# A hybrid Mamba, attention and expert kernel: arrival times in the plan of its prologue, a clearing moved to block 32, a root moved to block 13

## The chip, the cores and the metric

The kernel runs on one core of one Trainium2 chip. The metric is the time of one execution on the device, in microseconds. A core has five engines with a queue each, which work in order: TensorE (PE), VectorE (DVE), ScalarE (ACT), GpSimd (POOL) and SyncE (SP, which here only issues transfers). They wait for each other through semaphores.

## The reference

The input is an image batch x of shape (4, 256, 32, 32), used as 4 batches of 256 channels by N = 1024 positions. Two layers follow each other. What the change touches lies in the first third of layer 0; the rest is listed so that its place is clear.

```python
# layer 0, on the group-normalised x (32 groups of 8 channels)
xn = layernorm(xs, norm_w, norm_b)                  # over the 256 channels, per position
xc = xn in NB = 4 parts of DM = 64 channels
# mamba, for each part and batch: DIN = 128, DS = 16 states, K = 4 taps
u, z = split(xs @ inw.T)
u = silu(causal_conv(u, convw) + convb)
xdbc = u @ xpw.T
dt = softplus(xdbc[:DTR] @ dtw.T + dtb)
h_t = exp(dt_t * A) * h_{t-1} + dt_t * u_t * B_t    # the scan, over 1024 positions
y = (h_t summed with C_t over the states) + u * Dp
xm = (y * silu(z)) @ outw.T + skip_scale * xc
# a gate over the parts of a batch
Q = pointwise(depthwise_3_taps(x_concat));  xg = sigmoid(Q) * xm
# then: convolutions, attention with 8 heads, gelu, a depthwise 3 x 3 convolution, a projection
# layer 1: attention with softmax over 1024 positions, then 16 experts of which each token takes 2
```

## The kernel before

**The stages.** A prologue loads the inputs, normalises x and makes the first part's scan inputs (until about 88 us). A scan loop of 256 blocks follows (to about 1032 us); then come the convolutions and attentions and the experts, which the change doesn't touch.

**The scan loop.** A block is 8 of the 128 inner channels of one part of one batch, with 16 states each: 128 rows by 1024 positions. 16 blocks make a part, 64 a batch. In block t, DVE multiplies dBu by B (L976) and scans (L979), and POOL multiplies by C (L980). PE spreads dt * u over the states for block t + 2 (`select`, L919) and sums the states of block t - 3 (`add_up`, L930 and L937). ACT takes the exponential for block t + 3 (`decay`, L912), on data which SP fetches for block t + 4 (L907). Steps of the next parts (`front`) and of parts just ended are issued at fixed blocks between these, in program order: whatever is issued at a block stands on its engine's queue at that place. A list `behind` of pairs (block, step) holds what the prologue leaves to the loop. For batch 3 these are the variances of the layernorm (`var_late`, L742 and L780), their reciprocal root (`root`, twelve small DVE steps, L676 to L683), a diagonal matrix of them on POOL (L755), and the multiplications that apply it (L763 to L770).

**The gate.** When the four parts of a batch are done, `module_gate` computes the gate in blocks 5, 21 and 37 after the batch's end. Its step 0 first runs for batch 0 in block 85. PE projects (L600) and ACT writes three shifted copies (L603) into a tile of 96 rows by 1026 columns, `late_gate[0]`, of which only 4 rows in each 32 are written. The remaining rows and the edge columns have to be zero, and are set so once, by POOL (L596). The tile lies in the space where x of batch 3 was held; the last to read it there are the variances of block 8.

**The prologue.** Its instructions are not in the order of the text. Each step is handed to a planner with `add`, with the engine, a cost in ns, what it reads and writes, and an optional `lag` until the result is there. The class `Plan` simulates the engines with these costs and issues the steps in the order of their simulated starts. So the costs fix only the order on each queue; on the chip, semaphores set the times. There are three kinds of steps: `main` (the chain of batch 0: `normalise(0)` and `first_front`), `fill` (`weights`: constants made from loaded weights) and `low` (the other batches and the first matmuls of part 1). A fill step goes ahead when it ends before the next main step could start, plus 300 ns; a low step may hold up a main step of its engine by up to 700 ns. When the plan shows a hole on PE, `between` puts filler matmuls of the identity with itself there (L630), one for 330 ns of planned hole. Each of them shows as two records in the profile.

`normalise(b)` runs through: sums over positions on DVE (L694, one for each half k of the channels), a matmul over groups (L695), the negative mean (L696), squares on ACT (L700), a matmul over groups (L703), the root on DVE (L706 and the lines from L676), scaling (L712); then the layernorm over channels: mean by matmul (L723), subtraction (L727), squares (L732), variances (L742), the root (L751), the diagonal (L755), its replication (L795), and the products (L801 to L813). `weights` makes m_cu (`taps`, L823, from m_in and convr), m_first (L825), m_wdt (L830 on PE, L832 on DVE, from m_xp and m_dt), pick (L833), ddiag and sdiag (L835, L836, from the constants) and aneg (L837, L838). `first_front` goes from m_first and the normalised batch 0 to dt and to U, the input of `select` (L855 to L892), with transfers of dt (L873) and of the parts of U (L885).

The input transfers are all issued by SP, in the order of the text, and none by the planner. The plan is told of them by steps on SP that issue nothing: one for each batch of x, with lags 9500, 13000, 16000 and 19000 ns. Of the weights it is told nothing, so they count as there at time 0; `taps` alone waits for batch 0 in the plan.

Of the kernel before, what the change touches and what calls it, by code (L numbers as in the profile page):

```python
# [17 lines left out]
B, C, HH, WW = 4, 256, 32, 32  # L18
# [149 lines left out]
class Plan:  # L168
# [85 lines left out]
    def run(self):  # L254
        time = dict.fromkeys(self.LATENCY, 0.0)
# [52 lines left out]
        while left:  # L308
            choices = []
            for e in time:  # L310
                pick = self.choose(e, time[e], best, start)
                pick, kind = pick if pick is not None else (None, None)
                low = best(e, self.low.get(e, ()), "low", 40, lambda op: op["at"] <= self.position)
                if low is not None and (pick is None or low[0] + (0 if e == "DVE" and kind == "fill" else low[1]["ns"]) <= pick[0] + self.slack):
                    pick, kind = low, "low"
                if pick is not None:
                    wait = self.rather_act if e == "DVE" and pick[1]["other"] is not None else 0
                    choices.append((pick[0] + wait, pick[1]["n"], e, kind, pick[1], pick[0]))
            if not choices:

                nxt = [op["at"] for k in ("fill", "low") for ops in kinds[k].values() for op in ops if op["at"] > self.position]
                assert nxt, "the plan has a circle"
                self.position = min(nxt)
                continue
            _, _, e, kind, op, t = min(choices, key=lambda c: c[:2])
            for bank in op["banks"] if op["take"] else ():
                places = [(f, i) for i, f in enumerate(free) if f is not None]
                i = max(i for f, i in places if f <= t) if kind == "low" and self.split else min(places)[1]
                free[i] = None
                bank.t, bank.i, bank.kind = self.banks[i], i, kind  # L330
                taken[kind] += 1
            if e == "PE" and self.between is not None and time[e] > 0:
                for _ in range(int((t - time[e] - 100) // 330)):
                    self.between()
            if e == "PE":
                t += self.TURN * (op["tiled"] != self.tiled)
                self.tiled = op["tiled"]
            second = op["second"]
            if second is not None:
                free_at = max([d["end"] + self.LATENCY[d["engine"]] for d in second["deps"] if d["engine"] != e] + [t])  # L340
                op["emit"]()
                second["emit"]()
                op["end"] = t + op["ns"]
                time[e] = second["end"] = max(op["end"] + second["ns"], free_at + op["ns"])
                if second["pos"] is not None:
                    self.position = max(self.position, second["pos"])
                for o in (op, second):
                    kinds[kind][e].remove(o)
                left -= 2
                continue  # L350
            if op["other"] is not None:
                kinds[kind]["DVE" if e == "ACT" else "ACT"].remove(op)
                if e == "DVE":
                    op["engine"], op["ns"], op["emit"] = op["other"]
            op["emit"]()
            op["end"] = t + op["ns"] + op["lag"]
            time[e] = t + op["ns"]
            for bank in op["banks"] if op["give"] else ():
                free[bank.i] = op["end"] + self.LATENCY[e]
                taken[bank.kind] -= 1  # L360
            if op["pos"] is not None:
                self.position = max(self.position, op["pos"])
            kinds[kind][e].remove(op)
            left -= 1
# [31 lines left out]
def body(tc, g, out):  # L396
    nc = tc.nc
# [8 lines left out]
    with pool("const", 1) as cp, pool("dram", 1, space=bass.MemoryType.DRAM) as drp, contextlib.ExitStack() as late:  # L406
# [46 lines left out]
        with pool("mconst", 1) as mc, pool("front", 1) as fp, pool("dts", 2, space=bass.MemoryType.DRAM) as dsp, pool(  # L453
# [135 lines left out]
            def module_gate(b, step):  # L589

                q12 = late_gate[0]
                if step == 0:
                    if b == 0:
                        nc.gpsimd.memset(q12, 0.0)  # L596
                    p = big()
                    for h in HALVES:
                        for k in range(CT):
                            mm(p[:96, h], qdw[:, k, :], XM[b][:, k, XL + h.start : XL + h.stop], start=k == 0, stop=k == CT - 1)  # L600
                    for j in range(3):
                        rows_j = slice(32 * j, 32 * j + NB)
                        act(  # L603
                            q12[rows_j, 2 - j : 2 - j + N], p[rows_j], AF.Identity,
                            bias=V("qdw_b")[rows_j] if j == 1 else 0.0, scale=1.0,
                        )
                else:
                    k, t = step - 1, late_gate[1]
                    p = big()
                    for h in HALVES:  # L610
                        mm(p[:, h], qpw[:, k * P : (k + 1) * P], q12[:, 1 + h.start : 1 + h.stop], start=True, stop=True)
                    act(t, p, AF.Sigmoid, bias=V("qpw_b", k), scale=1.0)
# [7 lines left out]
            with pool("scan", 6) as sp, pool("yps", 1, space=PSUM) as yps, pool("dps", 2, space=PSUM) as dps, pool("lnA", 1) as wp:  # L620
# [64 lines left out]
                def normalise(b):  # L685
# [90 lines left out]
                    if b == B - 1:  # L776
                        def var_late():
                            p = big()
                            var(p)
                            nc.scalar.copy(small[:, 0], each(p))  # L780
                        behind.extend([(8, var_late), (10, root), (15, diagonal)])
                        late(22, 23, 24, 25, 27)
                        return
                    add("PE", 3500, lambda: var(bank.t), SQUARE(b), (), bank, take=True)
# [32 lines left out]
                def weights():  # L817
# [3 lines left out]

                    def taps():
                        tt(m_cu, m_in[:, :, 0:DIN].unsqueeze(2).to_broadcast([P, CT, K, DIN]), convr, ALU.mult)  # L823
                    add("DVE", 1270, taps, XS(0), ["m_cu"])
                    add("ACT", 700, lambda: nc.scalar.copy(m_first[0:DM], m_cu[0:DM, 0]), ["m_cu"], ["m_first"])  # L825
                    bank = pre.bank()

                    def low_rank():
                        for nb in range(NB):
                            mm(bank.t[:, nb * DIN : (nb + 1) * DIN], m_xp[:, nb], m_dt[:, nb], start=True, stop=True)  # L830
                    add("PE", 2000, low_rank, (), (), bank, take=True)
                    add("DVE", 690, lambda: nc.vector.tensor_copy(m_wdt, bank.t.rearrange("p (n d) -> p n d", n=NB)), (), ["m_wdt"], bank, give=True)  # L832
                    add("DVE", 420, lambda: nc.vector.tensor_copy(pick, pickf), (), ["pick"])  # L833
                    for nb in range(NB):
                        add("DVE", 150, lambda nb=nb: ts(ddiag[:, nb], ident, V("dd", nb), None, ALU.mult))  # L835
                    add("DVE", 150, lambda: ts(sdiag, ident, V("skip"), None, ALU.mult))  # L836
# [109 lines left out]
                fronts = [None] + fronts  # L946
                behind = []

                for b in range(B):
                    add("SP", 0, lambda: None, (), XS(b), lag=(9500, 13000, 16000, 19000)[b])  # L950
                with pre.beside(-1, -1, -1):
                    weights()
                normalise(0)
# [1160 lines left out]
```

## Time and profile before

| | |
|---|---|
| median of 3 runs | 2792.1 us (2788.51 to 2798.54) |
| profiled execution, its own time | 2778.86 us |
| its span, first to last instruction | 2776.9 us |
| prologue, to the first L976 | 87.78 us |
| scan loop, first L976 to last L979 | 87.78 to about 1034 us |
| mean granted TensorE clock | 0.968 |

In the lines of the profile, PE is the matmul, PEld the loading of its weights, L12 line 12 of the kernel; times are us. In a timeline each line has start, duration, engine, line, operation, output <- input, the shape, and a count where several alike follow each other. In brackets stands how long the engine was idle before, and what ended that. Where the letter q follows an engine's name, it is the engine's sequencer, which issues transfers and handles semaphores.

Busy time by stage (of the windows 0 to 40, 40 to 86, 86 to 150 and 150 to 220 us), in us:

| stage | length | PE | DVE | ACT | POOL |
|---|---|---|---|---|---|
| prologue, first part | 40 | 26.24 | 22.28 | 9.25 | 1.02 |
| prologue, second part | 46 | 42.23 | 33.14 | 32.82 | 16.55 |
| loop, first blocks | 64 | 44.59 | 58.24 | 42.59 | 47.61 |
| loop, after them | 70 | 61.25 | 64.30 | 45.20 | 62.32 |

### The profile page before, as it was taken

How to read it: one execution, taken by the hardware profiler on the slowest of the kernel's cores; microseconds unless marked ns; L12 is line 12 of the kernel's file. 1: busy time of each engine (PE TensorE's matmuls, PEld its weight loads, DVE VectorE, ACT ScalarE, POOL GpSimd, SP SyncE). 2: the span in 40 equal slices, each digit the busy share in tenths (PEclk: the TensorE clock that was granted, in tenths of full speed). 3: DMA queues.
4: the chain of work that ended last, by engine and by line, in shares of the span. 5: the costliest groups of instructions: out<-in, count | busy, mean ns of one | idle time of the engine just before them, and what ended most of it. 6: DMA issues, size and time to landing. Idle time of an engine off the chain costs nothing. (4 is left out here: it accounts for less than half of the span.)

```text
span 2776.9 us, 38965 instructions
## 1 busy us (share of the span) xinstructions
PE 2510.8 (90%) x15320; PEld 1494.1 (54%) x15320; DVE 1997.8 (72%) x2261; ACT 1540.8 (55%) x2082; POOL 1321.6 (48%) x822
## 2 busy tenths in 40 slices
PE   7788887888888878999999999999999998899996
PEld 5322222222223224675655565664666667899996
DVE  6899998999999987777985997777594556111112
ACT  4766766767767734666865975784543433112120
POOL 1788887998898870000010010012343336566652
PEclk9999999999999999999999999999999998999998
DMA  4667766787767743000001000000000014555546
GB/s 148 171 157 184 174 168 165 182 191 187 175 172 180 192 115 106 9 5 22 22 1 39 9 2 9 9 17 16 1 16 8 12 35 121 173 140 141 128 100 182
DMA packets 95433, 269.58 MB, mean 97 GB/s; under 512 B 18694, under 2 KB 36726, under 8 KB 91920
## 3 DMA queue, kind: packets, MB, share of 16 engines
q1 hardware_dynamic: 66560, 202.52, 28.6%
q0 software_dynamic: 26512, 60.35, 8.6%
q10 hardware_dynamic: 2176, 4.19, 0.4%
q8 instruction: 122, 2.00, 0.3%
q14 instruction: 63, 0.52, 0.1%
HBM read 291.57 MB, written 42.80 MB: 120 GB/s over the span
## 5 line engine op out<-in xcount | busy, mean ns | idle before, releaser
L980 POOL TENSOR_TENSOR hs<-hs,bc 128x1024 f32<-128x1024 f32 x256 | 600.5, 2360 | 122.3 <-DVE hs L979 119.9
L979 DVE TENSOR_TENSOR_SCAN hs<-dA,dBu 128x1024 f32<-128x1024 f32 x256 | 585.4, 2287 | 36.8 <-PE pY L937 2.2
L1322 DVE TENSOR_REDUCE nm<-s 128x1 f32<-128x1024 f32 x256 | 301.5, 1218 | 94.0 <-PE s L1313 90.1
L1327 ACT ACTIVATE pr<-s,nm 128x1024 f32<-128x1024 f32 x256 | 285.7, 1122 | 94.4 <-DVE nm L1322 69.5
L912 ACT ACTIVATE dA<-dA,aneg 128x1024 f32<-128x1024 f32 x256 | 285.9, 1143 | 86.7 <-DMA dA<-ds 83.3
L976 DVE TENSOR_TENSOR dBu<-dBu,bc 128x1024 f32<-128x1024 f32 x256 | 309.3, 1208 | 12.7 <-PE dBu L919 12.6
L1391 POOL TENSOR_TENSOR b<-b 128x1024 f32<-128x1024 f32 (+1 forms) x15 | 29.6, 1972 | 590.3 <-ACT b L1387 590.2
L1341 PE MATMUL k<-const,pr 128*128 128x128 f32 x2048 | 270.2, 278 | 20.4 <-ACT pr L1327 6.3
L1341 PEld LDWEIGHTS k<-const,pr 128*128 128x128 f32 x2048 | 226.5, 142 | 109.3 <-issue 48.0
L919 PE MATMUL dBu<-U,pick 96*128 96x512 bf16 x512 | 158.7, 393 | 111.6 <-DVE hs L979 111.4
L1989 PE MATMUL s<-pT,b 128*128 128x128 f32 x1920 | 231.3, 277 | 7.4 <-DMA b<-we,intse 6.2
L1989 PEld LDWEIGHTS s<-pT,b 128*128 128x128 f32 x1920 | 227.1, 193 | 12.6 <-issue 5.8
L1993 DVE TENSOR_TENSOR pT<-pT,s 128x512 f32<-128x512 f32 x72 | 49.4, 686 | 233.7 <-ACT pT L1992 233.6
L937 PE MATMUL pY<-hs,const 128*32 128x512 f32 x768 | 198.3, 639 | 0.0
L919 PEld LDWEIGHTS <-pick 96*128 96x128 bf16 x512 | 41.1, 99 | 282.2 <-issue 158.8
L1345 ACT COPY pT<-k 128x512 f32<-128x512 f32 x288 | 156.7, 597 | 51.7 <-PE k L1341 51.4
L1345 DVE COPY pT<-k 128x512 f32<-128x512 f32 x224 | 144.7, 682 | 33.8 <-PE k L1341 30.9
L1313 PE MATMUL s<-b,b 32*128 32x512 f32 x512 | 166.2, 646 | 0.7 <-ACT pr L1327 0.6
L1313 PE MATMUL s<-b,qs 32*128 32x512 f32 x512 | 166.2, 646 | 0.0
L930 PE MATMUL pY<-hs,const 128*128 128x512 f32 x256 | 139.6, 672 | 10.2 <-ACT u L568 7.7
L1361 PEld LDWEIGHTS k<-pT,b 128*32 128x32 f32 x4096 | 107.6, 110 | 59.2 <-issue 27.1
L1361 PE MATMUL k<-pT,b 128*32 128x128 f32 x4096 | 129.9, 276 | 3.0 <-DVE pT L1345 3.0
(485 smaller groups left out, 4645.5 us busy)
## 6 DMA issues: line engine op xcount, KB each, us to landing
dA<-ds SPq DMA_DIRECT2D x256, 512.0 KB, 5.6
dq<-parts SPq DMA_DIRECT2D x15, 768.0 KB, 3.7
U<-dq SPq DMA_DIRECT2D x45, 256.0 KB, 6.9
ds<-dt SPq DMA_DIRECT2D x16, 512.0 KB, 3.0
b<-x SPq DMA_DIRECT2D x4, 1024.0 KB, 6.9
acc<-pr SPq DMA_DIRECT2D x8, 512.0 KB, 7.5
qs<-b SPq DMA_DIRECT2D x32, 128.0 KB, 2.2
xm<-x SPq DMA_DIRECT2D x4, 1024.0 KB, 5.4
```

The costliest lines, as they stand in the source:

```text
L912: act(dAs[t], dAs[t], AF.Exp, scale=aneg[:, c : c + 1])
L919: mm(dBus[t][:, h], pick[:, j % 4], state[t // NJ]["U"][:, j // 4, h], start=True, stop=True)
L976: tt(dBu, dBu, r["B"], ALU.mult)
L979: nc.vector.tensor_tensor_scan(hs, dAs.pop(t), dBu, 0.0, ALU.mult, ALU.add)
L980: nc.gpsimd.tensor_tensor(hs, hs, r["C"], ALU.mult)
L1313: mm(S[i][:, HALVES[h]], q, kT[rr, HALVES[h]], start=True, stop=True)
L1322: "DVE", 1130, lambda i=i, u=u: nc.vector.tensor_reduce(nms[u], S[i], AX.X, ALU.max, negate=True),
L1327: "ACT", 1100, lambda i=i, u=u, hd=hd: act(prs[u % 4], S[i], AF.Exp, bias=nms[u], scale=1.0, accum_out=rss[b % 2][:, k, qt, hd : hd + 1]), ...
L1341: nc.tensor.transpose(bank.t[:, j * P : (j + 1) * P], prs[u][:, c0 : c0 + P], ident)
L1345: 470, 598, lambda dst=dst, bank=bank: nc.scalar.copy(dst, bank.t), lambda dst=dst, bank=bank: nc.vector.tensor_copy(dst, bank.t),
L1361: mm(bank.t[i * HD : (i + 1) * HD, 0:P], v[:, 4 * jh + j, hd * HD : (hd + 1) * HD], pTs[m][jh][:, i, j * P : (j + 1) * P], start=(jh, j) = ...
L1989: mm(p12[:, a, c], wbufs[w][:, o : o + P], xT[:, k], start=k == 0, stop=k == CT - 1)
```

## The change

It has three parts. First, the planner is told when each input arrives: x in halves, with its own time for each, and m_in, m_dt, convr and pick. `taps`, `low_rank` and the cast of pick wait for them in the plan. The transfers and their order are the same. Second, fillers may now also stand before the first step of PE, counted from 4500 ns on. Third, two steps move in the loop: the clearing of the gate tile from block 85 to block 32, and batch 3's root from block 10 to block 13.

```diff
-            if e == "PE" and self.between is not None and time[e] > 0:
-                for _ in range(int((t - time[e] - 100) // 330)):
+            if e == "PE" and self.between is not None:
+                for _ in range(int((t - max(time[e], 4500) - 100) // 330)):
                     self.between()
...
                 q12 = late_gate[0]
                 if step == 0:
-                    if b == 0:
-                        nc.gpsimd.memset(q12, 0.0)
                     p = big()
...
-                        behind.extend([(8, var_late), (10, root), (15, diagonal)])
+                        behind.extend([(8, var_late), (13, root), (15, diagonal), (32, lambda: nc.gpsimd.memset(late_gate[0], 0.0))])
...
-                    add("DVE", 1270, taps, XS(0), ["m_cu"])
+                    add("DVE", 1270, taps, ["m_in", "convr"], ["m_cu"])
...
-                    add("PE", 2000, low_rank, (), (), bank, take=True)
+                    add("PE", 2000, low_rank, ["m_dt"], (), bank, take=True)
...
-                    add("DVE", 420, lambda: nc.vector.tensor_copy(pick, pickf), (), ["pick"])
+                    add("DVE", 420, lambda: nc.vector.tensor_copy(pick, pickf), ["pickf"], ["pick"])
...
-                for b in range(B):
-                    add("SP", 0, lambda: None, (), XS(b), lag=(9500, 13000, 16000, 19000)[b])
+                for keys, ns in (
+                    (XS(0, [0]), 8000), (XS(0, [1]), 9400), (["m_in"], 10500), (["m_dt"], 11500), (["convr"], 12200), (["pickf"], 13000),
+                    (XS(1, [0]), 15300), (XS(1, [1]), 16600), (XS(2, [0]), 17900), (XS(2, [1]), 19200), (XS(3, [0]), 20500), (XS(3, [1]), 21500),
+                ):
+                    add("SP", 0, lambda: None, (), keys, lag=ns)
```

## Prediction

> **What bounds the kernel now.** I read the page first: the row of shares, then the slices. PE is busy 90% of the span, but that is an average over stages: in slices 1 to 15 it is DVE that stands at 9.
>
> ```profile
> PE 2510.8 (90%) x15320; PEld 1494.1 (54%) x15320; DVE 1997.8 (72%) x2261; ACT 1540.8 (55%) x2082; POOL 1321.6 (48%) x822
> PE   7788887888888878999999999999999998899996
> DVE  6899998999999987777985997777594556111112
> ```
>
> All three edits lie in the first 430 us, so PE's bound behind slice 16 is untouched: time saved before it moves the whole rest forward, time saved off the path there is worth nothing. The chain that ended last covers only the final 50 us and says nothing here. So I went to the timeline of the prologue, engine by engine, and to DVE's list of waits in the scan loop.
>
> The prologue, DVE and PE (start us, duration us, what, in brackets the idle time before and its releaser):
>
> ```profile
> 13.03 0.42 DVE L833 CAST pick<-sz 96x512 bf16<-96x512 f32 x1 [12.12 <-DMA sz<-pick]
> 15.05 2.33 DVE L694 TENSOR_REDUCE gst<-hs 128x1 f32<-128x1024 f32 x2
> 13.46 8.67 PE L630 MATMUL pY<-const 128*128 128x128 f32 x60
> 21.98 0.28 PE L695 MATMUL pY<-gst,const 128*128 128x2 f32 x2
> 22.29 0.16 DVE L696 TENSOR_SCALAR gst<-pY 128x2 f32<-128x2 f32 x1 [3.78 <-PE pY L695]
> 83.51 3.70 PE L484 MATMUL mm<-xm,m_cu 64*128 64x512 f32 x8
> 87.14 1.04 PE L919 MATMUL dBu<-U,pick 96*128 96x512 bf16 x4
> 87.78 1.23 DVE L976 TENSOR_TENSOR dBu<-dBu,bc 128x1024 f32<-128x1024 f32 x1 [1.69 <-PE dBu L919]
> ```
>
> To be seen: batch 0's sums (L694) stand on DVE's queue behind a cast that waits for the last small transfer, pick, until 13.03, though x of batch 0 is there at about 9.3 (issued from 1.66, 7.2 us median to landing). Then PE comes to their matmul (L695) only at 21.98, because 30 filler matmuls (60 records, two to one) stand before it. The scan loop starts at 87.78.
>
> The loop, at block 85 and at its counterpart one batch later:
>
> ```profile
> 422.94 0.95 POOL L596 MEMSET xs<- 96x1026 f32 x1
> 423.93 1.02 ACT L603 ACTIVATE xs<-mm 4x1024 f32<-4x1024 f32 x1 [6.54 <-POOL xs L596]
> 427.14 3.43 PE L544 MATMUL mm<-u,m_bc 128*128 128x512 f32 x4 [7.86 <-ACT xs L603]
> 431.04 1.23 DVE L976 TENSOR_TENSOR dBu<-dBu,bc 128x1024 f32<-128x1024 f32 x1 [7.81 <-PE dBu L919]
> ...
> 656.66 1.01 ACT L603 ACTIVATE xs<-mm 4x1024 f32<-4x1024 f32 x1
> 658.98 1.21 DVE L976 TENSOR_TENSOR dBu<-dBu,bc 128x1024 f32<-128x1024 f32 x1
> ```
>
> The memset waits in POOL's backlog, ACT for the memset, PE for ACT, DVE for PE. DVE loses 7.81 us. One batch later there is no memset and no gap.
>
> **Part 1, the prologue's plan.** The planner orders each queue by its own costs; I use those for order only and take durations from rows. Now x, m_in, m_dt, convr and pick carry arrival times, so on DVE only ddiag, sdiag and aneg precede the sums; these need const and vec, there at about 4.5 (ACT's aneg starts at 4.57 on vec). The second half of x0 lands at 9.3, its sum takes 1.17 (2.33 for two): 10.5. L695 takes 0.28, so L696 comes at about 10.9 instead of 22.29: **11.3 us earlier**. Taps, pick and m_wdt (1.21 + 0.42 + 0.68) move behind it, into the 2.4 us in which ACT squares batch 0 (two L700 rows), starting with convr at 12.2 (3.08 + 9.1); m_wdt waits for low_rank, 11.5 + 2.04 = 13.5, and ends by 14.4. L706, at 25.82 before, then comes at 14.4: still 11.4 earlier.
>
> Fillers: the first PE step is planned at 10.8, so (10800 - 4500 - 100)/330 = 18 fillers stand before L695, starting with const at 4.5. In the trace the first 9 of the 30 took 3.5 us (0.39 each), later ones 0.20: 9 × 0.39 + 9 × 0.20 = 5.3, ending near 9.9, under the wait for x0. If all 18 stayed slow they would end at 11.5: a loss of 1.0. The Trainium skill (TensorE: Matmul & The Clock Gate, "What's actually happening") says that the array falls to half clock after about 3.4 us idle and needs as long to come back. That speaks against this change: with x1 to x3 landing from 15.3 to 21.5 as before, PE has holes early. The nearest row: L495 took 3.78 at 94.44 after a gap, where the same four passes take 1.98 warm (L544 at 431.68). One such relapse costs 1.8 by row, up to 3.4 by the rule; fillers sit in every planned hole, so I take 0 and keep 3.4 for the range.
>
> What of the 11.4 survives to the loop? The other batches' work fills holes at lower priority. It can start at 15.4 instead of 22.37, only 7 us earlier, so it falls 4.4 us further behind. Two effects. (i) The first chain loses interruptions: the four L727 of batch 1 and two L696 which now stand before L755 (42.07 to 44.60) are not ready any more: 2.5 us gained. (ii) Displaced PE work piles up at the end. From L723 (30.43, will be 19.1) to 87.14 PE spends 56.7 us, of which 3.8 are fillers, some 2.5 idle, 50.4 work. In the new order I find holes of about 2 (before the variances L742), 3 (root and diagonal of batch 0, 2.5 + 1.2 less small matmuls), 1.8 (before L855) and up to 4 (the first select waits for U, which needs some 7 us from the last part to landing, with work queued behind it): 7 to 11. The last L484 then ends at 19.1 + 50.4 + 7 to 11 = 76.5 to 80.5 instead of 87.1. But the loop no longer waits for all of it: the first selects stand before the L484 and only block 2's stands behind. Block 3 needs last L484, table load 1.28, silu 1.11, L495 2.0 to 3.8, select 0.6: from 80.5 that is 85.5 to 87.3, against 99.12 (its L976 now): 11.8 to 13.6 earlier; from 76.5 DVE itself binds, at some 84. **I take -12.5** (ends -6, if all lag stays, and -15).
>
> **Part 2, the memset.** Gone from block 85: ACT, idle from 417.4, takes its three L603 at once (3.14 us), PE's L544 comes at 420.6 instead of 427.14, and the select is done as DVE ends its scan at 423.2. The counterpart at 656 stands in the same phase (L603 0.1 before a scan begins) and DVE waits nowhere there, but 0.5 three blocks later. So 7.81 - 0.2: **-7.6** (7.0 to 7.8). At block 32 it adds 0.95 to POOL, behind that block's L980:
>
> ```profile
> 219.22 2.36 POOL L980 TENSOR_TENSOR hs<-hs,bc 128x1024 f32<-128x1024 f32 x1 [1.12 <-DVE hs L979]
> 222.83 2.36 POOL L980 TENSOR_TENSOR hs<-hs,bc 128x1024 f32<-128x1024 f32 x1 [1.25 <-DVE hs L979]
> ```
>
> POOL idles 1.25 there, which covers it; its last reader, the variances of block 8, is long done. Without cover: 0.95, and behind it only the next L980. Cost 0.
>
> **Part 3, the root** of batch 3, from behind block 10 to behind block 13 on DVE.
>
> ```profile
> 129.85 0.58 DVE L676 TENSOR_SCALAR smalls<-smalls 128x8 f32<-128x8 f32 x1 [1.21 <-ACT smalls L780]
> 130.47 2.27 DVE L677 CAST smalls<-smalls 128x8 f32<-128x8 int32 x1
> 133.19 1.85 DVE L682 SCALAR_TENSOR_TENSOR smalls<-smalls 128x8 f32<-128x8 f32 x1
> 136.36 1.22 DVE L976 TENSOR_TENSOR dBu<-dBu,bc 128x1024 f32<-128x1024 f32 x1
> 129.45 0.60 PE L919 MATMUL dBu<-U,pick 96*128 96x512 bf16 x2
> ```
>
> The wait of 1.21 isn't saved: block 11's select (129.45 to 130.05) stands on PE behind the same variances, so DVE, free at 128.65, waits 1.4 for it. What can change is the 6.5 us that twelve steps of about 0.2 took: L676, L677 and L682 each ended with a POOL instruction. The Trainium skill (SBUF — State Buffer, "Who interferes with whom") says that such steps share a port with GpSimd and the later one waits out the other's whole instruction; it allows anything from 2.4 (POOL empty) to 2.4 plus every POOL instruction queued. Behind block 13, POOL, unstalled, still has L980 of 12, one L767 and L980 of 13 before it: root 140.6 to about 146, 5.5. So 6.5 - 5.5 - 0.2: **-1** (+1 to -4). The diagonal of block 15 follows that block's L980, after the root in any case.
>
> **Sum** against the profiled execution (span 2776.9, 2778.86 with what lies around): 12.5 + 7.6 + 1.0 = 21.1, giving 2757.8. The runs shown lie higher, median 2792.1 from 2788.5 to 2798.5, also without a change; the saved stretches are waits of DVE, so I subtract the same microseconds: **2771.0**.
>
> **Rivals.** (A) Full lag: the batches' work comes only as early as the prologue's end lets it, 6 us; sum 14.6, 2777.5. For: PE is packed from 30 to 87. Against: the interruptions lost, the loop's own start. (B) The prologue's gain is swallowed, by late U or relapsed clock, and only the memset remains: -7 to -8, 2784.5, within 0.3%. For: the first select waits for a transfer whose landing the plan puts at 2 us and the trace at 4.9. Against: everything upstream of U is earlier. (C) Slower: batches 2 and 3 are each processed behind the first chain, one after the other. One batch from its squares to its variances took 17 us (L700 at 22.49 to L742's end at 39.45); with the chain done near 68, 68 + 2 × 17 + 7.4 of L484 puts the loop at 109, 21.6 late: +13 after the other gains, 2805. It decides from 8.6 us of delay on. Against: DVE is free while the first chain sits in ACT, and the planner fills there. (D) The first chain keeps everything and DVE binds: -16 in the prologue, root at 2.5: sum 27, 2765.
>
> **Chances.** Forecast 0.62, A 0.17, D 0.11, B 0.06, C 0.04. A difference of 0.3% is what a measurement of this kernel can tell, 8.4 us. Forecast, A and D are beyond it: 0.90 faster, 0.06 same, 0.04 slower. The bounds give -14 to -27; with some 4 us for the spread of the runs, 2762 to 2781.
>
> **What the changed profile would show.** L696 near 11, L706 near 14.4, no L630 between const's landing and L695 beyond some 36 records. First L976 near 74, the fourth near 86. No ACT wait on L596 and no DVE gap near block 85; L596 between two L980 near 200. Root steps behind the scan of block 13, some of them stretched. It is wrong if the fourth L976 comes after 93, if L484 or L723 stand behind the first L919 in such number that DVE waits again in blocks 2 to 5, or if a gap reappears at block 85 with another releaser (U of the next module, or POOL's backlog, which loses its pause of 5.2).

## The result, and the profile after

The changed kernel takes 2807.9 us (median of 18 runs, 2795.8 to 2820.2), the kernel before on the same chip 2792.5 us (18 runs, 2787.8 to 2803.7). The ratio is 1.0047, with a 95% interval of 1.003 to 1.0065: 8 to 18 us slower. (The ratio is not that of the two medians, which lie 15.4 us apart.) The profiled execution took 2806.86 us, its span is 2804.5. In the changed kernel the loop's lines have moved: the product is L977 (L976 before), the scan L980, POOL's product L981, the select L917; the prologue's lines stand two lower (L692 for L694, L740 for L742).

The page of the changed kernel, shares and slices:

```profile
PE 2541.6 (91%) x15308; PEld 1506.1 (54%) x15308; DVE 2002.8 (71%) x2261; ACT 1538.3 (55%) x2081; POOL 1320.6 (47%) x822
PE   7788888888888978999999999999999997899996
DVE  5899999999989996777985997777584655211112
PEclk8899999999989999999999999999999999999998
```

PE is busy 31 us more than before with 12 instructions fewer: work at half clock counts as busy in full (below, 32 matmuls take 7.09 us instead of 3.68). PEclk, the clock that was granted to PE in tenths of full speed, has 8 in the first two slices, where the kernel before has 9.

The timeline of the prologue, DVE and PE, columns as before:

```profile
8.51 1.22 DVE L692 TENSOR_REDUCE gst<-hs 128x1 f32<-128x1024 f32 x1 [0.33 <-DMA hs<-x]
4.30 6.52 PE L628 MATMUL pY<-const 128*128 128x128 f32 x36 [4.30 <-DMA const<-const]
10.98 0.16 DVE L694 TENSOR_SCALAR gst<-pY 128x2 f32<-128x2 f32 x1 [1.24 <-PE pY L693]
14.02 0.16 DVE L704 COPY gst<-pY 128x2 f32<-128x2 f32 x1 [0.41 <-PE pY L701]
17.52 3.70 PE L721 MATMUL dBu<-hs,const 128*128 128x512 f32 x8 [0.34 <-DVE hs L710]
...
49.45 1.98 PE L721 MATMUL dBu<-hs,const 128*128 128x512 f32 x4
60.35 7.09 PE L740 MATMUL dBu<-const,xm 128*128 128x64 f32 x32 [2.46 <-ACT dBu L869]
67.57 1.28 DVE L870 TENSOR_TENSOR dt<-dt,dBu 128x512 f32<-128x512 f32 x2 [6.05 <-PE dBu L740]
88.24 1.22 DVE L977 TENSOR_TENSOR dBu<-dBu,bc 128x1024 f32<-128x1024 f32 x1
```

At the same steps the kernel before has, on PE:

```profile
39.29 1.94 PE L723 MATMUL pY<-hs,const 128*128 128x512 f32 x4
48.12 3.68 PE L742 MATMUL pY<-const,xm 128*128 128x64 f32 x32
```

The front is as forecast: batch 0's negative mean stands at 10.98, the start of its root at 14.02, its means for the layernorm at 17.52 (30.43 before). But batch 1's means come at 49.45, 10 us *later* than before (39.29), and its variances at 60.35 instead of 48.12, in 7.09 us instead of 3.68: the same 32 records at half clock. Then L870, the last step of dt in the first chain, waits 6.05 us for those variances, although it doesn't read them: they write the other half of the same PSUM tile, dBu (in the plan the two stand in places 2 and 3, the halves of one tile). Block 0 starts at 88.24, where it started before (87.78).

The same timeline from there, over the first blocks of the loop:

```profile
92.74 1.91 PE L793 MATMUL pY<-dA,const 128*128 128x512 f32 x2
98.67 1.88 PE L721 MATMUL pY<-xs,const 128*128 128x512 f32 x4
99.49 1.28 DVE L725 TENSOR_TENSOR xm<-hs,dBu 128x512 f32<-128x512 f32 x2 [2.89 <-ACT dA L807]
102.72 3.68 PE L740 MATMUL dBu<-const,hs 128*128 128x64 f32 x32
112.35 2.36 DVE L679 SCALAR_TENSOR_TENSOR smalls<-smalls 128x8 f32<-128x8 f32 x1
116.77 1.22 DVE L977 TENSOR_TENSOR dBu<-dBu,bc 128x1024 f32<-128x1024 f32 x1
```

Batch 1's replication, half of the means of batch 2 (the other half came at 83.23), the means of batch 3, the variances of batch 2 and their root run *inside* blocks 0 to 4. The kernel before had PE's share of this done at 83.6, ahead of its first select. The last line is block 4, 13.0 later than in the kernel before:

```profile
103.80 1.22 DVE L976 TENSOR_TENSOR dBu<-dBu,bc 128x1024 f32<-128x1024 f32 x1
```

Block by block the start is later by 0.5, 1.7, 7.1, 9.5 and 13.0.

The two moved steps, in the timeline of POOL and DVE:

```profile
230.31 2.36 POOL L981 TENSOR_TENSOR hs<-hs,bc 128x1024 f32<-128x1024 f32 x1 [1.13 <-DVE hs L980]
232.62 0.95 POOL L779 MEMSET xs<- 96x1026 f32 x1
233.92 2.35 POOL L981 TENSOR_TENSOR hs<-hs,bc 128x1024 f32<-128x1024 f32 x1 [0.36 <-DVE hs L980]
...
154.67 2.27 DVE L675 CAST smalls<-smalls 128x8 f32<-128x8 int32 x1
158.87 1.22 DVE L977 TENSOR_TENSOR dBu<-dBu,bc 128x1024 f32<-128x1024 f32 x1
...
432.15 1.21 DVE L977 TENSOR_TENSOR dBu<-dBu,bc 128x1024 f32<-128x1024 f32 x1
435.69 1.21 DVE L977 TENSOR_TENSOR dBu<-dBu,bc 128x1024 f32<-128x1024 f32 x1
```

The memset sits in a pause of POOL. Blocks 88 and 89 follow each other in 3.54 us, with no gap. Measured as the change of the lag against the kernel before, the gone gap is worth 12.55 - 4.65 = 7.9 us, and the root's move (-6.3 at block 11, +5.2 at block 14) 1.1 us.

The bill up to the loop's end: +13.0 at block 4, -1.1 and -7.9 for the moves, +8.6 in blocks 191 to 193 (the lag is 5.2 at block 190 and 13.8 at block 193), and about 3 in small steps give the +15.5 of block 255. The 8.6 are half clock again, with nothing of the change near it; the section on the hardware shows them. Behind the loop the profile loses another 12 us; there the kernel before was profiled in an execution 13 us below its own median, so I don't explain those 12.

### The profile page after: what moved, and what is told of

Same layout as the page of the kernel before. It is cut to its first block, busy times and chain, and to the rows that moved or that the text cites. A ratio compares the mean times of both kernels' runs of the same rounds, so it can differ in the third digit from the quotient of the medians.

```text
span 2804.5 us, 38932 instructions
## 1 busy us (share of the span) xinstructions
PE 2541.6 (91%) x15308; PEld 1506.1 (54%) x15308; DVE 2002.8 (71%) x2261; ACT 1538.3 (55%) x2081; POOL 1320.6 (47%) x822
## 3 DMA queue, kind: packets, MB, share of 16 engines
q0 software_dynamic: 26512, 60.35, 8.4%
## 5 line engine op out<-in xcount | busy, mean ns | idle before, releaser
L981 POOL TENSOR_TENSOR hs<-hs,bc 128x1024 f32<-128x1024 f32 x256 | 599.9, 2359 | 140.3 <-DVE hs L980 130.5
L980 DVE TENSOR_TENSOR_SCAN hs<-dA,dBu 128x1024 f32<-128x1024 f32 x256 | 585.3, 2286 | 39.9 <-PE pY L935 7.4
L1323 DVE TENSOR_REDUCE nm<-s 128x1 f32<-128x1024 f32 x256 | 301.4, 1217 | 94.7 <-PE s L1314 92.9
L977 DVE TENSOR_TENSOR dBu<-dBu,bc 128x1024 f32<-128x1024 f32 x256 | 309.5, 1209 | 12.4 <-PE dBu L917 12.3
L917 PE MATMUL dBu<-U,pick 96*128 96x512 bf16 x512 | 159.7, 395 | 111.7 <-DVE hs L980 107.9
L1990 PEld LDWEIGHTS s<-pT,b 128*128 128x128 f32 x1920 | 227.2, 193 | 11.4 <-issue 6.6
L935 PE MATMUL pY<-hs,const 128*32 128x512 f32 x768 | 206.3, 661 | 0.0
L917 PEld LDWEIGHTS <-pick 96*128 96x128 bf16 x512 | 41.3, 99 | 284.9 <-issue 159.6
L1346 ACT COPY pT<-k 128x512 f32<-128x512 f32 x288 | 156.6, 596 | 53.2 <-PE k L1342 52.9
```

Source lines behind the costliest of these rows:

```text
L935: mm(r["pY"][32 * q : 32 * q + 32, h], strip[:, P - DB - i * DB : P - i * DB + 32 - DB], hs[:, h], start=False, stop=False,)
L977: tt(dBu, dBu, r["B"], ALU.mult)
L980: nc.vector.tensor_tensor_scan(hs, dAs.pop(t), dBu, 0.0, ALU.mult, ALU.add)
L981: nc.gpsimd.tensor_tensor(hs, hs, r["C"], ALU.mult)
L1323: "DVE", 1130, lambda i=i, u=u: nc.vector.tensor_reduce(nms[u], S[i], AX.X, ALU.max, negate=True),
L1346: 470, 598, lambda dst=dst, bank=bank: nc.scalar.copy(dst, bank.t), lambda dst=dst, bank=bank: nc.vector.tensor_copy(dst, bank.t),
```

## The experiments

The readings in the table come from the profiles: the starts of blocks 0 and 4, the lag of block 255's start behind the kernel before (1030.6), and the mean granted clock from 40 to 90 us. One profile is one execution, and it can lie well off its kernel's median: that of the kernel before is 13 us below it, that of e2 12 and that of f1 15. So block 0, block 4 and the clock say where a kernel gains or loses, and the ratios whether it is faster. The medians are of 7 to 18 runs; the kernels ran on different chips, and each ratio is to the kernel before on the same chip.

| kernel | block 0 | block 4 | block 255 | clock 40-90 | median us | ratio, 95% |
|---|---|---|---|---|---|---|
| before | 87.8 | 103.8 | 0 | 1.00 | | |
| after | 88.2 | 116.8 | +15.5 | 0.83 | 2807.9 | 1.0047 (1.0030-1.0065) |
| e1 moves only | 89.4 | 105.9 | +6.1 | 1.00 | 2785.7 | 0.9974 (0.9951-0.9997) |
| e2 plan only | 89.5 | 116.7 | +17.4 | 0.83 | 2811.7 | 1.0053 (1.0030-1.0076) |
| e3 after, fit | 77.9 | 108.8 | -4.5 | 0.97 | 2778.4 | 0.9947 (0.9922-0.9972) |
| e4 after, dense fillers | 94.9 | 123.2 | +11.3 | 0.83 | 2802.4 | 1.0034 (1.0011-1.0056) |
| f1 after, 1400 ns | 92.9 | 108.1 | -5.5 | 0.97 | 2790.4 | 1.0008 (0.9990-1.0026) |
| f2 after, fit, 1400 ns | 97.4 | 112.6 | +10.5 | 0.97 | 2790.7 | 1.0012 (0.9994-1.0031) |
| f3 moves, fit | 89.7 | 106.4 | -4.2 | 1.00 | 2777.6 | 0.9961 (0.9939-0.9984) |
| f4 after, no shared tile | 69.6 | 114.3 | -0.3 | 0.86 | 2785.5 | 1.0001 (0.9983-1.0019) |
| g1 after, no fillers | 88.8 | 117.4 | +15.9 | 0.74 | 2799.1 | 1.0029 (1.0012-1.0047) |
| g2 before, no fillers | 85.2 | 101.3 | -2.5 | 0.96 | 2786.1 | 1.0005 (0.9980-1.0030) |
| g3 after, no early fillers | 89.9 | 117.3 | +4.5 | 0.83 | 2795.4 | 1.0027 (1.0004-1.0051) |
| g4 after, old times of x | 92.5 | 112.2 | +2.3 | 0.94 | 2793.1 | 1.0013 (0.9990-1.0036) |
| h1 after, fit, no fillers | 82.0 | 114.2 | +2.2 | 0.88 | 2791.2 | 0.9974 (0.9953-0.9995) |
| h2 moves, no fillers | 85.3 | 101.5 | +2.6 | 0.95 | 2793.2 | 0.9983 (0.9962-1.0004) |
| h3 moves, fit, no fillers | 87.9 | 103.8 | -9.8 | 0.93 | 2780.3 | 0.9942 (0.9917-0.9968) |

### Which part costs: e1 and e2

e1 is the kernel before with the memset and the root moved; e2 is the changed kernel with both put back.

```diff
 # e1, on the kernel before
-                    if b == 0:
-                        nc.gpsimd.memset(q12, 0.0)
...
-                        behind.extend([(8, var_late), (10, root), (15, diagonal)])
+                        behind.extend([(8, var_late), (13, root), (15, diagonal), (32, lambda: nc.gpsimd.memset(late_gate[0], 0.0))])
```

> The kernel before with the clearing moved to block 32 and the root to block 13, and the prologue's plan as it was. In the changed kernel the difference of block starts fell by 7.9 us at block 85 and by 6.3 - 5.2 = 1.1 us around blocks 10 to 13, so if the moves are independent of the plan: -9.0 us, about 2783.5 against 2792.5, first block at 87.8, no change at block 192. Rival: the half clock that cost 8.6 us at blocks 191 to 193 comes from the moves (they shift PE's phase in the loop); then it shows here too, and the time is within 1 us of before.

> The changed kernel with the clearing back in block 85 and the root back at block 10: only the prologue's plan and the early fillers are new. If the prologue alone makes the loss: block 4 starts 13 us later than before (116.8 against 103.8), and the time is 15.4 + 9.0 = 24 us above before, some 2817. Rival (the loss lies in the loop, by half clock, and the plan is about even): block 4 within 3 us of before, time within 8 us.

The moves alone are faster, by 1 to 14 us in the times; in the profile the gap at block 85 is again worth 7.9. (Its lag of +6.1 at the end holds 9.0 us of half clock at blocks 127 to 129, which the section on the hardware shows.) The plan alone is slower, 8 to 21 us, and has block 4 at 116.7 as the changed kernel has. The whole loss is the prologue's plan, with its early fillers.

### What of the plan: e3 and e4

The planner looks at the low steps (the other batches' work) of an engine, takes the one that could start first, and drops the idea altogether if that one would hold up the main chain for more than 700 ns. In e3 it takes the first low step that fits instead. e4 leaves the plan alone and puts more fillers into PE's planned holes.

```diff
 # e3
-                low = best(e, self.low.get(e, ()), "low", 40, lambda op: op["at"] <= self.position)
-                if low is not None and (pick is None or low[0] + (0 if e == "DVE" and kind == "fill" else low[1]["ns"]) <= pick[0] + self.slack):
-                    pick, kind = low, "low"
+                low = None
+                for op in self.low.get(e, ())[:40]:
+                    t = start(op, "low", e) if op["at"] <= self.position else None
+                    if t is None or low is not None and low[0] <= t:
+                        continue
+                    if pick is None or t + (0 if e == "DVE" and kind == "fill" else op["ns"]) <= pick[0] + self.slack:
+                        low = (t, op)
+                if low is not None:
+                    pick, kind = low, "low"
 # e4
-                for _ in range(int((t - max(time[e], 4500) - 100) // 330)):
+                for _ in range(int((t - max(time[e], 4500) - 100) // 200)):
```

> The changed kernel, but a low step that doesn't fit no longer hides the low steps behind it in the planner's list: the first that fits is taken. Theory lag (batches 2 and 3 fell behind because batch 1's scaling, 2.1 us, stood at the head of the list and never fitted): their means and squares come some 10 us earlier, at most one layernorm is left for blocks 0 to 4, and block 4 starts at 100 to 106 instead of 116.8: time 10 to 16 us below the changed kernel. Theory clock (PE is slow because of holes, whatever the order): block 4 stays above 112, granted clock in 40 to 90 us below 0.9, time within 5 us of the changed kernel.

> The changed kernel with one filler for 200 ns of planned hole on PE instead of 330, so that planned holes are filled whole. Theory clock: the granted clock in 40 to 90 us rises from 0.83 to above 0.95, the variance matmuls of batch 1 take 3.7 instead of 7.1 us, block 4 starts 4 to 8 us earlier, time 4 to 8 us lower. Theory lag: the clock may rise, but block 4 moves by less than 3 us and the time by less than 3; fillers that overrun a hole can make it later.

e3 has block 0 at 77.9 and block 4 at 108.8, and is faster than both kernels: 0.9947. So a low step that is too long for a hole kept short ones out of it: in the plan, batch 1's root and scaling on DVE (2100 and 820 ns) kept back the negative means of batches 2 and 3 (160 ns). Yet the 10 us that block 0 gains, and 5 more, are spent by block 4: batch 1's replication, batch 2's variances and its root still stand behind the first select. e4 loses another 6.4 us by block 4 and its clock stays at 0.83 where above 0.95 was expected: more fillers add work and don't raise the clock.

### Who goes first: f1, f2, f3

f1 is the changed kernel in which a low step may hold up a main one by 1400 ns instead of 700, f2 adds the choice of e3 to that. f3 is e1 with the choice of e3.

```diff
 # f1, f2
-                add, pre.spare, pre.slack, pre.split = pre.add, (2, 3), 700, True
+                add, pre.spare, pre.slack, pre.split = pre.add, (2, 3), 1400, True
```

> The changed kernel; a low step may hold up a main step of its engine by 1400 ns instead of 700. In the planned order no layernorm work is left behind the first select on PE. Theory lag: the first chain becomes later (dt goes out at 70 to 76 instead of 68.9), and yet block 4 comes earlier, at 98 to 104 instead of 116.8, since nothing is left for blocks 0 to 4; time 2770 to 2780, below the kernel before. Theory first chain (block 4 follows the moment at which dt goes out): a later chain gives a later block 4, above 117, and a time above the changed kernel.

> Both planner edits together: 1400 ns, and the first low step that fits. Theory lag: as with 1400 alone, block 4 at 96 to 104, time 2766 to 2778; where the two differ, the one whose PE has fewer holes between 20 and 80 us is earlier. Theory first chain: block 4 above 117.

> The kernel before with the two moves and with the choice of the first low step that fits, but with the old arrival times and no early fillers. If the new choice alone is what helped the third experiment, the time falls here too, to about 2775 (7 us under the moves alone). Theory lag: in the old order nothing was left behind the first select, so there is nothing to gain: within 4 us of the moves alone (2785.7), block 4 within 3 us of theirs (105.9).

The timeline of f1, DVE and PE:

```profile
64.86 3.79 PE L740 MATMUL dBu<-const,hs 128*128 128x64 f32 x32
74.16 1.98 PE L721 MATMUL dBu<-xs,const 128*128 128x512 f32 x4 [0.71 <-DVE smalls L749]
92.91 1.23 DVE L977 TENSOR_TENSOR dBu<-dBu,bc 128x1024 f32<-128x1024 f32 x1 [11.43 <-PE dBu L917]
108.11 1.22 DVE L977 TENSOR_TENSOR dBu<-dBu,bc 128x1024 f32<-128x1024 f32 x1
```

Here the low work is done ahead of the loop (batch 2's variances at 64.86, the last means at 74.16), so blocks 0 to 4 take 15.2 us (16.0 before, 28.5 after). The price stands in the third line: the first chain comes late, and DVE waits 11.43 us for the first select. Block 4 is 8.7 us earlier than after, but short of the 98 to 104 that was expected, and the time is that of the kernel before (1.0008), not below it. f2, which does both, has block 0 at 97.4 and block 4 4.5 us later than f1. So either the first chain or the other batches pays. f3 shows that the choice doesn't speed the old order: block 4 is at 106.4, 0.5 later than in e1, and the times don't tell the two apart (0.9961 and 0.9974, with intervals that overlap).

### The shared tile: f4

In f4 no low step gets the half of a PSUM tile whose other half a main step holds, and a main step takes a tile in which no low step holds a half where there is one (lines left out below).

```diff
-                open_ = sorted(f for f in free if f is not None)
+                open_ = sorted(f for i, f in enumerate(free) if f is not None and not (kind == "low" and shared(i)))
...
+        holder = {}
+
+        def shared(i, kind="main"):
+            return i < 4 and free[i ^ 1] is None and holder.get(i ^ 1) == kind
...
                 free[i] = None
+                holder[i] = kind
```

> The changed kernel, but the planner gives a low step no half of a PSUM tile whose other half a main step holds, and main steps avoid halves beside low ones. It takes away what made the last step of dt (L870) wait 6.05 us for the variances of batch 1, which wrote the other half of the same tile. Theory sharing (that wait is what the change loses): dt goes out near 62, block 4 at 104 to 110, time 7 to 12 us below the changed kernel. Theory lag: dt goes out near 62, but the low steps find fewer places, more of them come behind the first select, and block 4 stays at 113 or later, time within 5 us of the changed kernel or above.

The timeline of f4, whose select is L925, variances L748, means L729, product L985:

```profile
68.88 0.59 PE L925 MATMUL dBu<-U,pick 96*128 96x512 bf16 x2 [0.17 <-issue]
69.58 1.23 DVE L985 TENSOR_TENSOR dBu<-dBu,bc 128x1024 f32<-128x1024 f32 x1
74.07 6.93 PE L748 MATMUL pY<-const,xm 128*128 128x64 f32 x32
102.61 3.61 PE L729 MATMUL pY<-xs,const 128*128 128x512 f32 x4 [5.60 <-DVE xs L718]
114.28 1.22 DVE L985 TENSOR_TENSOR dBu<-dBu,bc 128x1024 f32<-128x1024 f32 x1
```

This is the clearest of all: the first chain keeps more than everything that was forecast for it, block 0 starts 18.2 us earlier than before, and block 4 is 10.5 us late all the same. The blocks in between take 44.7 us, because batch 1's variances come at 74.07 and batch 3's means at 102.61. The 6 us wait for the tile was real, and with it gone block 4 is only 2.5 us earlier than after. The times say more: 1.0001 against 1.0047. In the profile the other 13 us of block 255's lag come later: 3 in small steps by block 89, and 10 behind it, 8.6 of which are the half clock of blocks 191 to 193 that this execution didn't meet. So sharing was wrong on the place and right on the time, and I can't say which part of the time the tile itself is worth.

### The clock: g1, g2, g3, h1

g1, g2 and h1 issue no fillers (`self.between()` becomes `pass`) in the changed kernel, the one before, and e3. g3 takes out the early ones alone.

```diff
 # g3, on the changed kernel
-            if e == "PE" and self.between is not None:
-                for _ in range(int((t - max(time[e], 4500) - 100) // 330)):
+            if e == "PE" and self.between is not None and time[e] > 0:
+                for _ in range(int((t - time[e] - 100) // 330)):
```

> The changed kernel without any filler matmul (before and after have 120 to 132 records of them before the loop, 17.9 to 21.0 us of PE). Theory clock (PE's idle time up to block 4 is 26.2 us after and 26.5 before; the 13 us lie in PE's busy time, 90.5 against 77.3, from work at half clock, which fillers fail to prevent but limit): without them more work falls to half clock, block 4 starts at 118 to 126, granted clock from 40 to 90 us below 0.80, time 3 to 10 us above the changed kernel's. Theory order (the other batches' work is left behind the first chain and must be done before block 4 whatever the clock): fillers lie in holes only, block 4 at 114 to 119. Theory fillers in the way: block 4 at 112 or earlier.

> The kernel before without any filler matmul. Theory clock: the plan before kept full clock to 90 us because its holes were filled; without fillers the granted clock from 20 to 90 us falls to 0.85 or less and block 4 starts at 108 to 116 instead of 103.8, up to the place where the changed kernel has it. Theory order: the order of the work is the one before, so block 4 stays within 103 to 106.

> The changed kernel without the fillers ahead of PE's first step (36 records, 6.5 us, from 4.3 to 10.8 us). Theory clock: the first work runs at half clock, the first sums' chain loses 1 to 3 us and block 4 starts at 117 to 120. Theory order: nothing waits for PE there, block 4 at 115 to 118. If these fillers themselves cost: block 4 at 114 or earlier.

> The changed kernel with the planner's choice of the first low step that fits, and without fillers. With the choice alone: block 0 at 77.9, block 4 at 108.8, granted clock 0.97 from 40 to 90 us. Theory order (the left-behind work costs what it costs, the clock adds little): block 4 at 105 to 110 although the clock falls. Theory clock (the choice helped because it closed PE's holes, which kept the clock): without fillers the clock from 40 to 90 us is 0.85 or less and block 4 at 112 to 118, block 0 at 80 or later.

Busy time by engine in a stretch (PE, PEld, DVE, ACT, POOL, each with its instructions), then granted clock, DMA share and GB/s. First g2:

```profile
0.00:40.00 40.00, 16.87 (x66) 11.02 (x67) 25.63 (x71) 10.04 (x17) 1.02 (x13) 1.00 0.72 256
40.00:90.00 50.00, 41.77 (x146) 21.35 (x145) 34.59 (x86) 36.58 (x54) 17.62 (x14) 0.96 0.30 73
```

The same of e3, and below it of h1:

```profile
40.00:90.00 50.00, 42.06 (x147) 20.96 (x146) 35.18 (x75) 31.11 (x46) 15.04 (x13) 0.97 0.37 90
```

```profile
40.00:90.00 50.00, 40.07 (x106) 17.45 (x105) 35.96 (x75) 31.57 (x46) 12.84 (x11) 0.88 0.33 79
```

In the old order block 4 doesn't need the fillers: without them it comes 2.5 us earlier, at a clock of 0.96 from 40 to 90 us. The 1.00 in the first row of g2 is not to be taken at its word. The eight matmuls of batch 0's means, first in the kernel before, then in g2:

```profile
30.43 3.60 PE L723 MATMUL dBu<-hs,const 128*128 128x512 f32 x8
```

```profile
25.23 5.17 PE L723 MATMUL dBu<-hs,const 128*128 128x512 f32 x8 [0.37 <-DVE hs L712]
```

PE was slower there without fillers, though the clock's row shows nothing of it; from 40 us on the row and the durations agree (L795 takes 3.48 us at 42.24, where the row has 0.50). So fillers did speed up the first matmuls of the old order, and block 4 had no use for it.

In the changed kernel their loss costs clock (0.83 to 0.74) and 0.7 us, and leaving out the early ones alone costs 0.5. So neither they nor their lack made the loss. But h1 has the same order as e3, and there the fall from 0.97 to 0.88 goes with 5.4 us at block 4. The theory of the clock had said 112 to 118, though at a clock of 0.85 or less. The clock counts, then, in this order. The sizes are an estimate from single profiles that differ in their fillers too: from after (116.8, mean clock up to block 4 0.85) to h1 (114.2 at 0.84) 2.6 us are order at equal clock; from h1 to e3 (108.8 at 0.90) 5.4 are clock, more if leaving out fillers saves here what it saved before; the last 5.0 to the kernel before (103.8 at 0.96) are the low steps that e3 still leaves behind the first select, with what is left of the clock. No run separates the two further.

### Which arrival time: g4

g4 is the changed kernel with the old times for x (9500, 13000, 16000 and 19000 ns, each for a whole batch), the new ones for m_in, m_dt, convr and pick.

```diff
-                    (XS(0, [0]), 8000), (XS(0, [1]), 9400), (["m_in"], 10500), (["m_dt"], 11500), (["convr"], 12200), (["pickf"], 13000),
-                    (XS(1, [0]), 15300), (XS(1, [1]), 16600), (XS(2, [0]), 17900), (XS(2, [1]), 19200), (XS(3, [0]), 20500), (XS(3, [1]), 21500),
+                    (XS(0), 9500), (["m_in"], 10500), (["m_dt"], 11500), (["convr"], 12200), (["pickf"], 13000),
+                    (XS(1), 13000), (XS(2), 16000), (XS(3), 19000),
```

> The changed kernel with the old arrival times of x in the plan (9500, 13000, 16000 and 19000 ns, each for a whole batch), the new ones of m_in, m_dt, convr and pick kept. Theory order: the sums of the other batches count as there 2.3 to 3.5 us earlier, go further forward in the order and less of their work is left behind the first chain; block 4 at 104 to 111. Theory first chain (it is the earlier start of batch 0 alone that pushes the others back, by its place in the order): block 0's half arrivals differ by 0.1 to 1.5 us only, block 4 at 114 to 119. Theory clock says nothing on the order; where the clock from 40 to 90 us stays at 0.83, block 4 is at 113 or later, where it is above 0.95, at 108 or earlier.

Block 4 at 112.2 lies between both expectations: by this one profile the true times of x cost 4.5 of the 13 us, and the rest comes with the other times and the early fillers. The split is not settled by it, since the ratios of g4 and of the changed kernel have intervals that overlap.

### A faster version: h2 and h3

Both are e1 without fillers, h3 also with the choice of e3.

> The kernel before with the memset and the root moved and without fillers. Theory sum (each part as measured alone: fillers -2.5 at block 4, memset -7.9, root -1): block 4 at 101 to 103, last block 9 to 12 us earlier than before, 2777 to 2783 in time. Theory clock: the moves shorten waits in which PE worked; without fillers the clock of the prologue falls below 0.9 and block 4 lies at 105 or later.

> The same with the planner's choice of the first low step that fits. Theory sum: it was 106.4 at block 4 with fillers, so 102 to 105 without; last block 5 to 10 us earlier than before, 2774 to 2781 in time, not above the kernel with fillers (2777.6). Theory clock: block 4 at 107 or later, time 2780 or more.

By block 4 h2 is the sum of its parts (-2.3 where they give -2.5), by block 89 it is not (-8.1 where they give -11.4); then half clock at blocks 127 to 129 takes 9.0 us. It ends the loop 2.6 us late where 9 to 12 early was expected, and its time isn't distinguishable from that of the kernel before. h3 ends the loop 9.8 us earlier, within what was expected, and is, with e3, the fastest against its own comparison: 0.9942, 9 to 23 us faster than before. Between h3, e3 and f3 the intervals overlap; that h3 is the best of them isn't shown.

## Why the prediction was wrong

**The front, right.** L696 at 10.9 was forecast and is at 10.98 (now L694); L706 at 14.4 and is at 14.02. The 18 early fillers (36 records) end at 10.82, not 9.9: 0.36 each, as the slow first ones were. So the matmul of the sums starts at 10.66 where the second sum ends at 9.73, a loss of 0.9; its bound was given as 1.0. That L696 came on time all the same is luck: the second half of x was there by 8.5 us and not at 9.3, which made up for the fillers.

**What survives to the loop, wrong, and this is the step that failed.** I wrote that the other batches' work "falls 4.4 us further behind", and kept its order: last L484 at 76.5 to 80.5, everything else ahead of it. The last L484 does end at 77.8, but it is no longer last. With other arrival times the planner drew up another order, in which the low work fell some 23 us behind the chain (batch 1's means 10.2 later, the chain's 12.9 earlier) and batch 1's replication, the variances and root of batch 2 and most of the means of batches 2 and 3 went behind the first select. Two of the prediction's own signs of being wrong were there: the fourth product at 108.64, beyond 93, and L721 (its L723) behind the first select. I had worked out where the *chain* goes from the plan's rule, and where the *low work* goes from the old trace. e2 shows that the plan alone does it, and e3, f1 and f4 show the mechanism: start the chain earlier and low work pays, let low work in and the chain pays; by block 4, f4 gives back 28.7 us of lead.

**The half clock, wrong: "I take 0 and keep 3.4 for the range".** Holes of 7 to 11 us in PE were forecast; PE idles 10.7 of the 50 us from 40 to 90 (5.6 before). The changed kernel's profile has a clock of some 0.50 from 60 to 74 us and again behind 80.6, 91.9 and 112.3, each time after a hole on PE: 2.46, 2.22, 5.92 and 3.29 us. The rule of the Trainium skill (TensorE: Matmul & The Clock Gate, "What's actually happening") that I weighed and set aside was right in sign, but not in length: three of these four holes are shorter than its 3.4 us. One relapse was to cost 1.8 to 3.4 and there were several. Counted up to block 4, PE is idle 26.2 us, as before (26.5); the 13 us lie in its busy time, 90.5 against 77.3. The fillers are 21.0 against 17.9 of it. The rest, 69.5 us in 225 records against 59.4 in 221, is nearly the same work, done more slowly. Such a sum doesn't say how much of the 10 us block 4 waited for; h1 against e3 puts the clock's part at 5.4 in their order. The two failures hang together, since the new order is what placed the holes.

**A wait that I didn't see.** L870 standing 6.05 us behind the variances in the other half of its tile was in no part of the sum. It needs the order of the low work, which I had wrong. It works both ways: the variances themselves had stood 2.46 us behind ACT's step on dt's half (L869), and that hole is the one in front of their half clock.

**Memset and root, right.** -7.6 (7.0 to 7.8) was forecast and -7.9 measured; -1 and -1.1; the root's 5.5 us were 5.2, with one step of 2.27 and one of 0.97 among those of 0.17.

**Rivals.** C, "batches 2 and 3 are each processed behind the first chain", is what happened, at 2807.9 where it said 2805, and had a chance of 0.04. The objection to it, "the planner fills there", was false: the planner fills with the one low step that could start first, or with none. Its place was wrong too: the batches don't hold back the loop's start but run inside blocks 0 to 4, at 13 us instead of 21.6, and half clock later on (8.6 us) made up for what the moves gained. So its time was met by luck.

**Sums.** Two terms of the prediction are off, and neither bears on the result: the parts of D give 26.1 and not 27, and from 30.43 to 87.14 PE was busy 52.9 us, so it idled 3.8 and not 2.5, which leaves 49.0 of work besides 3.9 of fillers instead of 50.4.

## What to carry to other kernels

A plan that gives one chain priority moves the rest of the work, not just the chain: before costing a change of its inputs, redo the order of the low work with the planner's own rule, and look for the last of it, not the first of the chain. Measure such a change at the first point behind which the loop runs steadily (here block 4): at block 0 f4 would have looked like a gain of 18 us. And a helper that was put in for a reason, like the fillers, is worth a run without it.

## What was unexpected of the hardware

Half clock comes without a long hole. The timeline of PE in the changed kernel, and below it at the same place in the kernel before:

```profile
797.99 1.01 PE L917 MATMUL dBu<-U,pick 96*128 96x512 bf16 x2 [1.29 <-DVE hs L980]
798.93 3.63 PE L935 MATMUL pY<-hs,const 128*32 128x512 f32 x8
802.49 3.78 PE L484 MATMUL mm<-xm,m_cu 64*128 64x512 f32 x4
807.16 7.19 PE L484 MATMUL mm<-xm,m_cu 64*128 64x512 f32 x8
```

```profile
792.82 0.59 PE L919 MATMUL dBu<-U,pick 96*128 96x512 bf16 x2 [1.27 <-DVE hs L979]
793.35 1.91 PE L937 MATMUL pY<-hs,const 128*32 128x512 f32 x8
795.19 1.98 PE L484 MATMUL mm<-xm,m_cu 64*128 64x512 f32 x4
797.63 3.70 PE L484 MATMUL mm<-xm,m_cu 64*128 64x512 f32 x8
```

Both follow a hole of the same length, 1.29 and 1.27 us. The kernel before runs on at full clock, the changed one some 20 us at half (granted 0.87 from 790 to 800 us, 0.50 to 810, 0.60 to 820), and DVE then waits 4.44 us for one select. It happened at blocks 191 to 193 after, at 127 to 129 in e1 and h2, at 111 to 113 in g1, at 47 to 49 in f2: each time just where a part begins and three groups of L484 are issued, and at 8.1 to 9.0 us each. What sets it off stays open; no run here tells.

The clock shows in the times. Over 35 runs of the kernel before on one chip, the mean granted clock went from 0.957 to 0.969 and the time from 2806 to 2778: 2.0 us for each 0.001, with a correlation of -0.93. The median of the clocks was 0.965 before, on this chip and two others, and 0.9565 after, on the chip of the result; at that slope 0.0085 is 17 us, the size of the whole difference. But the slope doesn't hold from one kernel to another: h3, with a median clock of 0.9605 against 0.966 of the kernel before on its chip, should be 11 us slower by it, and is the fastest in the table by its ratio. Nor is a low clock a loss wherever it stands: from 90 to 150 us the kernel before has 0.83 too. That the order lowers the clock is shown for the prologue (0.83 from 40 to 90 us in after, e2, e4 and g3 alike), and only argued for the rest.
